# A four-layer graph network on one Trainium2 core: masks made early, mask bytes from the cast adjacency, keys centred in two operations, and three buffers or queues moved

## The chip, the core and the metric

The kernel runs on one core of one Trainium2 chip. The engines are TensorE (PE in the profile; its weight loads have a row of their own, PEld), VectorE (DVE), ScalarE (ACT), GpSimd (POOL) and SyncE (SP), which issues DMAs. DMAs are issued by SP, ACT and POOL, each in the order of its own queue. The metric is the device time of one execution in microseconds (us), lower is better. "L538" is line 538 of the kernel before.

## What is computed

Input are x (4096 nodes, 256 features) and adj (4096 x 4096, zeros and ones, about 0.8% ones). Four layers follow each other, each with a residual and a layernorm:

```python
x = layernorm(x + gat(x, W, b, a, adj))          # layer 0
x = layernorm(x + (diag(adj) + adj) @ (x @ w) + bias)   # layer 1
x = layernorm(x + two_steps(x, adj, W1, W2, W3, U1, U2)) # layer 2
x = layernorm(x + relu([x, mean_of_neighbours(x)] @ W + b)) # layer 3

# layer 0: 8 heads of 32 columns
logits[i, j, h] = leaky_relu(parent[i, h] + child[j, h], 0.2)
logits = where(adj[i, j] != 0, logits, 0)        # not minus infinity
out[i, h] = sum_j softmax_j(logits)[i, j, h] * feats[j, h]

# layer 2, twice: Xf = R @ Xf ; Xa = top_p_attention(Xa) @ Xa
# logits = (Xa W1' W2') (Xa W3')' ; keep the most probable 0.9 of each row
# Z += Xf @ U1[n].T + Xa @ U2[n].T
```

## The kernel before, in words

Nodes are handled in 32 blocks of 128 rows (NB). A scheduler of the framework puts the instructions of the Python program on each engine's queue, in an order of its own outside the parts marked as scheduled by hand; buffers of a pool are reused in rotation (`bufs`), and an instruction waits until the buffer it writes is free.

**Layer 0, sums0 (L404).** First the node features: for each pair of blocks (L443 to L483), x is loaded (SP, tile "x", three buffers), transposed by PE (L451), copied by ACT (L453), and multiplied with w0 (L457), whose logit columns DVE makes from the weights (L431, L432). `row_logits` stores one row of logits per head to memory (lpd).

Then the adjacency pass (L518 to L553): for each pair of blocks b, eight chunks g of four column blocks. Each chunk is loaded by SP into one of two "a" slots (L526), cast to the matmul's type by DVE (`ar`, L528, two buffers), turned to mask bytes by ACT (`nb`, L531, two instructions), which POOL stores to memory (`nad`, L532), and used by 32 matmuls of PE (L538). `factored` (L499 to L515) splits the weighted features of a block into three bf16 parts: DVE and ACT take turns (L503 to L513, tiles `vf` and `gb`, two buffers each), and ACT issues two stores per block (`gmd`, L515). The scheduler places these 32 blocks within 72 to 230 us. At the end of a pair, DVE combines the sums (`zt`, L547 to L552) and ACT stores them (`zd`, L553).

The mask of a chunk of attention (`mask`, L256 to L270) is: compare a row of logits with four column logits (DVE L261 for g of 2, 5, 7; otherwise ACT L267, a Sign), then one bitwise operation of DVE with the bytes (L263 or L269). `chunk0`, called near the end of the pass (L540), makes the mask of chunk 0 of head 0 ahead; it borrows both "a" slots, and its result is `gt0`, with the features in `gm0`.

**choose0 (L356)** branches on a value in memory (L358); all engines take part. Then the **attention loop** (L287 to L340): two halves of four heads; within a half, four tiles of 1024 rows (it); within it, four heads (hh); within a head, eight chunks g of 32 matmuls each (L320). At a tile's start SP loads bytes (`na`, L291) and, for it = 0, features (`gm`, L293) in the order of g. DVE reduces and normalises (L326 to L337). Layernorms that are due (`later`) are done one per head: DVE takes moments (L85, L86), POOL does the rest (L88, L89, L96), in tiles of two buffers (moments, L77).

**Layer 1 (L754)** multiplies by the adjacency, block by block (L787 to L799), with a layernorm on each (L798, tiles in the pool "l1w"; here DVE does L96 and POOL L88, L89). **Layer 2 (L802)** begins with `weights(0)` (L1519 to L1524: POOL issues loads of wt and affine) and `keys(0, X)`. `keys` (L877) transposes X (PE L901, ACT copies L902 to tile "e"), projects it (L906), and takes the moments of the keys: 32 matmuls (L923), DVE L924, PE L928, DVE L929 (`mom`). Then it centres them: for each of four parts of 1024 columns, DVE subtracts the mean in place (L935), ACT rounds to the matmul's type (L936, upper half of kT), and DVE takes the remainder (L937, lower half). PE's logits for the first rows (L979) read kT. `project` (L1445 to L1481) makes projections of two blocks; block 16 is projected before the centring, blocks 18 on in a loop (L1587). The main part of layer 2 (L1623 on) is scheduled by hand. Step 1 repeats keys. Layer 3 follows (L1845).

Of the kernel before, what the change touches and what calls it, by code (L numbers as in the profile page):

```python
# [9 lines left out]
F32 = mybir.dt.float32  # L10
I32 = mybir.dt.int32
F32R = mybir.dt.float32r
BF16 = mybir.dt.bfloat16
FP8 = mybir.dt.float8e4
# [9 lines left out]
P = 128  # L24
# [31 lines left out]
class Net:  # L56
# [19 lines left out]

    def moments(self, pool, src):  # L77

        nc = self.nc
        n = src.shape[1]  # L80
        stats = pool.tile([P, n, nc.vector.BN_STATS_DIM], F32, name="ln_stats")
        mv = pool.tile([P, n, nc.vector.BN_AGGR_DIM], F32, name="ln_mv")
        rstd = pool.tile([P, n], F32, name="ln_rstd")
        for q in range(n):
            nc.vector.bn_stats(stats[:, q, :], src[:, q, :])  # L85
            nc.vector.bn_aggr(mv[:, q, :], stats[:, q, :])  # L86
        var = pool.tile([P, n], F32, name="ln_var")
        nc.gpsimd.tensor_scalar_add(var, mv[:, :, 1], EPS)  # L88
        nc.gpsimd.tensor_tensor(rstd, var, self.power.to_broadcast([P, n]), ALU.pow)  # L89
        return mv, rstd  # L90

    def layernorm(self, pool, dst, src, engine=None):

        mv, rstd = self.moments(pool, src)
        for q in range(src.shape[1]):
            (engine or self.nc.vector).tensor_scalar(dst[:, q, :], src[:, q, :], mv[:, q, 0:1], rstd[:, q:q + 1],  # L96
                                                     op0=ALU.subtract, op1=ALU.mult)
# [117 lines left out]
    def layer0(self):  # L215
# [7 lines left out]
        with ExitStack() as ctx:  # L223
# [14 lines left out]
            first = pool.tile([P, IT], F32, name="lpb0")  # L238
            gt0 = pool.tile([P, 4, IT], FP8, name="gt0")
            gm0 = pool.tile([P, 4, 6 * C1], BF16, name="gm0")  # L240

# [5 lines left out]

            def chunk0(work):

                nc.sync.dma_start(gm0, gmd[0, :, 0:4, 0])  # L250
                na0, sg0 = (work.tile([P, 2, 4, P], F32, name="a", bufs=2).rearrange("p q k i -> p (q k i)").bitcast(U8)
                            .rearrange("p (k i) -> p k i", k=4) for _ in range(2))
                nc.sync.dma_start(na0, nad[0, :, 0:4, :])
                mask(gt0, sg0.bitcast(FP8), na0, first, 0, 0)

# [15 lines left out]

            self.sums0(both, nlc, fac, lpd, nad, zd, gmd, lambda: row_logits(first, 0, 0), chunk0)
            self.choose0(fac, zd, gmd, gm0)
# [13 lines left out]
            for half in range(2):  # L287
                for it in range(N // IT):
                    i0 = it * Q
                    for g in range(NB // K):  # L290
                        nc.sync.dma_start(na[:, g * K:(g + 1) * K], nad[it, :, g * K:(g + 1) * K, :])  # L291
                        if it == 0 and (half or g):
                            nc.sync.dma_start(gm[:, g * K:(g + 1) * K, 0], gmd[half, :, g * K:(g + 1) * K, 0])  # L293
# [8 lines left out]
                    for hh in range(H // 2):  # L302
# [5 lines left out]
                        for g in range(NB // K):  # L308

                            head0 = half == 0 and hh == 0 and g == 0  # L310
                            gt = gt0
                            if not head0 or it:
                                gt = work.tile([P, K, IT], FP8, name="gt", bufs=4)
                                sg = work.tile([P, K, IT], FP8, name="sg", bufs=3)
                                mask(gt, sg, na[:, g * K:(g + 1) * K, :], lpb, g, h)
                            for k in range(K):
                                jc = g * K + k
                                for q in range(Q):

                                    nc.tensor.matmul(acc[:, q, :6 * C1], gt[:, k, q * P:(q + 1) * P],  # L320
                                                     gm0[:, k, :] if head0 else gm[:, jc, hh, :],
                                                     start=(jc == 0 and q % 2 == 0),
# [15 lines left out]
                        for xs in later[:per_head]:  # L338
                            self.layernorm(work, xs, xs, nc.gpsimd)
                        del later[:per_head]  # L340
# [62 lines left out]

    def sums0(self, both, nlc, fac, lpd, nad, zd, gmd, then, chunk0):  # L404

# [5 lines left out]
        with ExitStack() as ctx:  # L411
# [31 lines left out]
            for b in range(0, NB, 2):  # L443
                two = slice(b, b + 2)
                x = work.tile([P, 2, D], F32, name="x", bufs=3)
                nc.sync.dma_start(x, xr[:, two, :])
                px = ps.tile([P, 512], F32, name="ps_x", bufs=2)
# [51 lines left out]
            def factored(b):  # L499
# [14 lines left out]
                for half in range(2):  # L514
                    nc.scalar.dma_start(gmd[half, :, b], gb[:, half * H // 2:(half + 1) * H // 2].rearrange("p h s c -> p h (s c)"))  # L515

            G = 4
            for b in range(0, NB, 2):  # L518
# [4 lines left out]
                for g in range(NB // G):  # L523
                    a = work.tile([P, 2, G, P], F32, name="a", bufs=2)
                    for q in range(2):
# [4 lines left out]
                    for q in range(2):  # L530
                        nc.scalar.mul(nb[:, :, q, :], a[:, q], float(FIFTH))  # L531
                    nc.gpsimd.dma_start(nad[it, :, g * G:(g + 1) * G, i:i + 2 * P], nb.rearrange("p g q i -> p g (q i)"))  # L532
                    for q in range(2):
                        for k in range(G):
                            jc = g * G + k
                            for s in range(2):
                                for t in range(2):
                                    nc.tensor.matmul(pz[q][:, t, :W], ar[:, q, k, :], src[:, jc, t, s],  # L538
                                                     start=(jc == 0 and s == 0), stop=(jc == NB - 1 and s == 1))
                if b == NB - 4:  # L540
                    chunk0(work)
                for q in range(2):
# [9 lines left out]
                    nc.vector.tensor_add(zt[:, 0], zt[:, 0], zt[:, 1])  # L552
                    nc.scalar.dma_start(zd[b + q], zt[:, 0])  # L553

# [199 lines left out]
    def layer1(self):  # L754
        nc, tc, NB, D, X = self.nc, self.tc, self.NB, self.D, self.X
        with self.ctx1 as ctx:
# [25 lines left out]
            for b in range(NB):  # L782
# [14 lines left out]
                nc.vector.tensor_add(xb[:, 0], xb[:, 0], row)  # L797
                self.layernorm(work, xb, xb)  # L798
                nc.gpsimd.dma_start(self.xd[b, :, 0, :], xb[:, 0])  # L799


    def layer2(self):  # L802
# [3 lines left out]
        with ExitStack() as ctx:  # L806
# [70 lines left out]
            def keys(step, src):  # L877
# [17 lines left out]
                for g in range(NB // 4):  # L895
# [23 lines left out]
                    for t in range(2):  # L919
                        nc.sync.dma_start(qd[t * A:(t + 1) * A, :, cols], qp)  # L920
                pm = ps1.tile([P, 512], F32, name="ps_r")
                for b in range(NB):
# [7 lines left out]

                project(step, 16)
                for c in range(N // 1024):
                    cols = slice(c * 1024, (c + 1) * 1024)
                    kc = qs[:A, cols]
                    nc.vector.tensor_scalar(kc, kc, mom[:A, 2 * A:], None, op0=ALU.subtract)  # L935
                    nc.scalar.copy(kT[:A, cols], kc)  # L936
                    nc.vector.tensor_sub(kT[A:, cols], kc, kT[:A, cols].bitcast(F32))  # L937
                pc = psum.tile([P, 512], F32, name="ps_tp")
# [580 lines left out]
            def weights(step):  # L1519

                ut = (self.u1t, self.u2t)[step]
                for i in range(2):
                    nc.gpsimd.dma_start(wt[:, :, i], ut[1 - i].rearrange("(c p) m -> p c m", p=P))
                nc.gpsimd.dma_start(affine, row_broadcast((self.ln_b, self.ln_g)[step], D))  # L1524

# [38 lines left out]
            for step in range(2):  # L1564
# [14 lines left out]
                for b in range(0, NB, 2):  # L1579
# [3 lines left out]
                    if edge:  # L1583
                        v = result(edge)
                        if v is not None:
                            rs[0], edge = v, None
                    if b:  # L1587
                        project(step, (b + 16) % NB)
# [367 lines left out]
```

## Time and profile before

| what | us |
|---|---|
| median of three executions | 4033.21 (4031.47 to 4039.32) |
| the profiled execution itself | 4036.06 |
| its span on the core | 4034.4 |
| PE busy | 3912.9 (97%) |
| DVE busy | 2994.1 (74%) |
| ACT busy | 2757.1 (68%) |
| POOL busy | 1088.5 (27%) |
| node features | 0 to 62 |
| adjacency pass | 72 to 600 |
| attention | 603 to 1327 |
| layer 1 | 1327 to 1625 |
| layers 2 and 3 | 1625 to 4034 |

The page sums busy time per engine over the span. The table of waits sums PE's idle time by the instruction that ended it. The timeline lists instructions in order of their start; the last bracket gives the idle time of the engine just before, and what released it. A row with "x32" joins 32 instructions in a row. The letter q after an engine (SPq) means its queue, where DMAs are issued. The granted clock of PE is 0.987 of full speed over the span.

### The profile page before, as it was taken

How to read it: one execution, taken by the hardware profiler on the slowest of the kernel's cores; microseconds unless marked ns; L12 is line 12 of the kernel's file. 1: busy time of each engine (PE TensorE's matmuls, PEld its weight loads, DVE VectorE, ACT ScalarE, POOL GpSimd, SP SyncE). 2: the span in 40 equal slices, each digit the busy share in tenths (PEclk: the TensorE clock that was granted, in tenths of full speed). 3: DMA queues.
4: the chain of work that ended last, by engine and by line, in shares of the span. 5: the costliest groups of instructions: out<-in, count | busy, mean ns of one | idle time of the engine just before them, and what ended most of it. 6: DMA issues, size and time to landing. Idle time of an engine off the chain costs nothing. (4 is left out here: it accounts for less than half of the span.)

```text
span 4034.4 us, 68767 instructions
## 1 busy us (share of the span) xinstructions
PE 3912.9 (97%) x25081; PEld 3383.5 (84%) x25081; DVE 2994.1 (74%) x6643; ACT 2757.1 (68%) x5127; POOL 1088.5 (27%) x1333
## 2 busy tenths in 40 slices
PE   8999999999999999899999999989999999999899
PEld 7899999999999788578888888865888888888687
DVE  7642328999999444567878788737899999999364
ACT  5543339999999322468888888825988888888132
POOL 0111110111333122301111111114555555555211
PEclk9999999999999999999999999999999999999999
DMA  4665547334222597432333232453333333335541
GB/s 136 224 214 175 178 147 228 93 101 131 69 76 64 192 369 311 131 115 95 98 97 101 95 104 92 146 190 100 103 116 103 106 119 99 107 120 188 185 152 47
DMA packets 320570, 556.42 MB, mean 138 GB/s; under 512 B 71558, under 2 KB 146198, under 8 KB 316118
## 3 DMA queue, kind: packets, MB, share of 16 engines
q1 hardware_dynamic: 239920, 395.13, 30.2%
q0 software_dynamic: 28336, 86.42, 6.5%
q10 hardware_dynamic: 51958, 70.29, 5.1%
q8 instruction: 203, 3.33, 0.3%
q14 instruction: 153, 1.25, 0.1%
HBM read 385.78 MB, written 165.94 MB: 137 GB/s over the span
## 5 line engine op out<-in xcount | busy, mean ns | idle before, releaser
L1345 PE MATMUL ps_a<-X,aT 128*128 128x256 f32 x4096 | 973.4, 380 | 1.3 <-ACT h L1486 1.1
L1345 PEld LDWEIGHTS ps_a<-X,aT 128*128 128x128 f32 x4096 | 776.5, 190 | 128.2 <-issue 3.5
L320 PE MATMUL acc<-gm,gt 128*128 128x198 bf16 x8192 | 706.2, 249 | 22.0 <-DMA gm<-gmd 6.8
L320 PEld LDWEIGHTS <-gt 128*128 128x128 fp8e4 x8192 | 702.8, 98 | 25.4 <-issue 9.8
L267 ACT ACTIVATE sg<-lpb,nlc 128x1024 fp8e4<-128x1024 f32 x636 | 667.2, 1135 | 61.5 <-DVE gt L269 39.8
L180 PE MATMUL ps_r<-XD,adj_piece 128*128 128x512 f32 x1888 | 528.4, 414 | 0.3 <-DMA adj_piece<-adjs 0.3
L538 PE MATMUL pz<-src,ar 128*128 128x264 f32 x4096 | 510.2, 287 | 15.2 <-DVE ar L528 12.7
L538 PEld LDWEIGHTS pz<-src,ar 128*128 128x128 f32 x4096 | 507.1, 190 | 18.1 <-DVE ar L528 11.6
L1072 ACT ACTIVATE ja<-e,nc 128x2048 uint8<-128x2048 f32 x240 | 480.9, 2004 | 2.0
L1338 ACT COPY aT<-ps_tp 128x512 f32<-128x512 f32 x512 | 296.4, 579 | 222.5 <-PE ps_tp L1336 220.5
L180 PEld LDWEIGHTS ps_r<-XD,adj_piece 128*128 128x128 f32 x1888 | 332.9, 189 | 69.3 <-issue 12.9
L531 ACT ACTIVATE nb<-a 128x512 uint8<-128x512 f32 x256 | 156.4, 630 | 287.7 <-DMA a<-in_adjt_dram 274.7
L1137 DVE MAX8 cand<-v 128x8 f32<-128x256 f32 x1024 | 347.3, 412 | 4.4
L1187 DVE SCALAR_TENSOR_TENSOR e<-e,edge 128x512 f32<-128x512 f32 x512 | 347.3, 750 | 2.2
L1336 PE MATMUL ps_tp<-ident,e 128*128 128x128 f32 x2048 | 307.9, 273 | 0.0
L1133 DVE SCALAR_TENSOR_TENSOR v<-e,hi 128x2048 f32<-128x2048 f32 x128 | 300.7, 2350 | 2.4
L1336 PEld LDWEIGHTS ps_tp<-ident,e 128*128 128x128 f32 x2048 | 257.1, 142 | 51.4 <-issue 0.7
L261 DVE TENSOR_SCALAR sg<-lpb,nlc 128x1024 fp8e4<-128x1024 f32 x384 | 285.4, 779 | 5.9 <-DVEq L358 3.9
L979 PE MATMUL ps_logit<-kT,q 128*128 128x512 f32 x1024 | 276.8, 412 | 12.4 <-DVE kT L937 8.0
L981 ACT ACTIVATE e<-ps_logit 128x1024 f32<-128x1024 f32 x256 | 260.2, 1027 | 30.3 <-PE ps_logit L979 30.3
L528 DVE CAST ar<-a 128x1024 fp32r<-128x1024 f32 x128 | 88.6, 693 | 231.0 <-PE pz L538 229.9
L790 PE MATMUL ps_adj<-XD,adj_piece 128*128 128x512 f32 x1024 | 244.9, 399 | 0.0
(397 smaller groups left out, 5543.7 us busy)
## 6 DMA issues: line engine op xcount, KB each, us to landing
adj_piece<-adjs SPq DMA_DIRECT2D x552, 256.0 KB, 2.7
a<-in_adjt_dram SPq DMA_DIRECT2D x256, 256.0 KB, 3.0
adjs<-adj_piece SPq DMA_DIRECT2D x96, 512.0 KB, 4.8
na<-nad SPq DMA_DIRECT2D x64, 512.0 KB, 3.7
nad<-nb POOLq DMA_DIRECT2D x128, 128.0 KB, 3.3
lpb<-lpd POOLq DMA_DIRECT2D x32, 512.0 KB, 4.1
na<-nad ACTq DMA_DIRECT2D x16, 1024.0 KB, 6.9
gmd<-gb ACTq DMA_DIRECT2D x64, 198.0 KB, 3.3
```

The source lines that it names most:

```text
L180: nc.tensor.matmul(ps, a[:, k, :], rhs(jc).rearrange("p s d -> p (s d)"), start=(jc == 0), stop=(jc == self.NB - 1))
L261: nc.vector.tensor_scalar(sg[:, k, :], lpb, nlc[:, 4 * g + k, h:h + 1], 2.0 ** -5, op0=ALU.is_ge, op1=ALU.mult, saturate=False)
L267: nc.scalar.activation(sg[:, k, :], lpb, AF.Sign, scale=-1.0, bias=nlc[:, 4 * g + k, h:h + 1], saturate=False)
L320: nc.tensor.matmul(acc[:, q, :6 * C1], gt[:, k, q * P:(q + 1) * P], gm0[:, k, :] if head0 else gm[:, jc, hh, :], start=(jc == 0 and q % 2 ...
L538: nc.tensor.matmul(pz[q][:, t, :W], ar[:, q, k, :], src[:, jc, t, s], start=(jc == 0 and s == 0), stop=(jc == NB - 1 and s == 1))
L1072: nc.scalar.activation(ja, e[:, s * HALF:(s + 1) * HALF], f, bias=nc1, accum_out=fs[:, i + s:i + s + 1])
L1133: nc.vector.scalar_tensor_tensor(v, ec, hi, ec, op0=ALU.is_lt, op1=ALU.mult, accum_out=sb[:, s:s + 1])
L1137: nc.vector.max(cand[:, 8 * j:8 * j + 8], v[:, k * 256:(k + 1) * 256])
L1187: nc.vector.scalar_tensor_tensor(ec, ec, edge[:, j:j + 1], ec, op0=ALU.is_ge, op1=ALU.mult)
L1336: nc.tensor.transpose(pt[:, k * P:(k + 1) * P], e[:, jc * P:(jc + 1) * P], self.ident)
L1338: nc.scalar.copy(aT, pt)
L1345: nc.tensor.matmul(pa[:, :D], aT[:, k * P:(k + 1) * P], X[:, jc, :], start=(jc == 0), stop=(jc == NB - 1))
```

## The change

1. x is loaded into the "a" slots, four blocks to a tile by two DMAs; the tile "x" is gone. "a" still has two buffers.
2. nb is made from ar, the cast adjacency, and not from a.
3. POOL and not ACT issues the gmd stores of `factored`.
4. `early_mask` takes the place of `chunk0`: it makes the masks of chunks 0 and 1 of head 0 in four parts of two column blocks, at b = 20 to 26, by DVE alone, in the tiles "nf" and "v"; `gt0` and `gm0` hold eight column blocks and not four.
5. In the attention loop's first tile, SP loads chunks 2 to 7 first and then 0 and 1; chunks 0 and 1 of the first head use gt0 and gm0; `gm` of chunk 0 is loaded in both halves.
6. The layernorm tiles of `later` in the attention loop have six buffers.
7. The last two zd stores are issued by SP.
8. Layer 1's layernorm on each block takes its tiles from the pool "l1" (one buffer by default, two for these tiles).
9. In `keys`, ACT makes the upper half of kT by an Identity with the negated mean as its bias, straight from qs; DVE makes the lower half in one operation (subtract the mean, subtract the upper half). `project` of blocks 16 and 18 stands ahead of the moments.
10. `weights(0)` is issued by SP and not by POOL; `weights(1)` as before.

```diff
-    def moments(self, pool, src):
+    def moments(self, pool, src, bufs=2):
...
-        stats = pool.tile([P, n, nc.vector.BN_STATS_DIM], F32, name="ln_stats")
+        stats = pool.tile([P, n, nc.vector.BN_STATS_DIM], F32, name="ln_stats", bufs=bufs)
...
+            def early_mask(work, part):
+
+                if part == 0:
+                    nc.sync.dma_start(gm0, gmd[0, :, 0:8, 0])
+                two = slice(2 * part, 2 * part + 2)
+                na0, sg0 = (work.tile([P, 2, H, C1], F32, name=name).rearrange("p s h c -> p (s h c)")[:, :512]
+                            .bitcast(dt).rearrange("p (k i) -> p k i", k=2) for name, dt in (("nf", U8), ("v", FP8)))
+                nc.sync.dma_start(na0, nad[0, :, two, :])
+                for k in range(2):
+                    nc.vector.tensor_scalar(sg0[:, k, :], first, nlc[:, 2 * part + k, 0:1], 2.0 ** -5,
+                                            op0=ALU.is_ge, op1=ALU.mult, saturate=False)
+                bits = [t.rearrange("p k i -> p (k i)").bitcast(U32) for t in (gt0[:, two, :], sg0, na0)]
+                nc.vector.tensor_tensor(*bits, ALU.bitwise_and)
...
-                    for g in range(NB // K):
+                    begun = 2 if it == half == 0 else 0
+                    for g in [*range(begun, NB // K), *range(begun)]:
                         nc.sync.dma_start(na[:, g * K:(g + 1) * K], nad[it, :, g * K:(g + 1) * K, :])
-                        if it == 0 and (half or g):
+                        if it == 0:
                             nc.sync.dma_start(gm[:, g * K:(g + 1) * K, 0], gmd[half, :, g * K:(g + 1) * K, 0])
...
-                            head0 = half == 0 and hh == 0 and g == 0
-                            gt = gt0
-                            if not head0 or it:
+                            head0 = g < 2 and half == it == hh == 0
+                            if head0:
+                                gt = gt0[:, g * K:(g + 1) * K, :]
+                            else:
...
-                            self.layernorm(work, xs, xs, nc.gpsimd)
+                            self.layernorm(work, xs, xs, nc.gpsimd, bufs=6)
...
-                x = work.tile([P, 2, D], F32, name="x", bufs=3)
-                nc.sync.dma_start(x, xr[:, two, :])
+                if b % 4 == 0:
+                    x4 = work.tile([P, 2, 4, P], F32, name="a").rearrange("p q k i -> p (q k i)").rearrange(
+                        "p (b d) -> p b d", d=D)
+                    for q in range(0, 4, 2):
+                        nc.sync.dma_start(x4[:, q:q + 2], xr[:, b + q:b + q + 2, :])
+                x = x4[:, b % 4:b % 4 + 2]
...
-                    nc.scalar.dma_start(gmd[half, :, b], gb[:, half * H // 2:(half + 1) * H // 2].rearrange("p h s c -> p h (s c)"))
+                    nc.gpsimd.dma_start(gmd[half, :, b], gb[:, half * H // 2:(half + 1) * H // 2].rearrange("p h s c -> p h (s c)"))
...
-                        nc.scalar.mul(nb[:, :, q, :], a[:, q], float(FIFTH))
+                        nc.scalar.mul(nb[:, :, q, :], ar[:, q].bitcast(F32), float(FIFTH))
...
-                if b == NB - 4:
-                    chunk0(work)
+                if NB - 12 <= b < NB - 4:
+                    early_mask(work, (b - NB + 12) // 2)
...
-                    nc.scalar.dma_start(zd[b + q], zt[:, 0])
+                    (nc.sync if b == NB - 2 else nc.scalar).dma_start(zd[b + q], zt[:, 0])
...
-                self.layernorm(work, xb, xb)
+                self.layernorm(pool, xb, xb)
...
+                for b in (16, 18):
+                    project(step, b)
                 pm = ps1.tile([P, 512], F32, name="ps_r")
...
-                project(step, 16)
+                minus = kept[:A, 130:131]
+                nc.vector.tensor_scalar_mul(minus, mom[:A, 2 * A:], -1.0)
                 for c in range(N // 1024):
                     cols = slice(c * 1024, (c + 1) * 1024)
-                    kc = qs[:A, cols]
-                    nc.vector.tensor_scalar(kc, kc, mom[:A, 2 * A:], None, op0=ALU.subtract)
-                    nc.scalar.copy(kT[:A, cols], kc)
-                    nc.vector.tensor_sub(kT[A:, cols], kc, kT[:A, cols].bitcast(F32))
+                    nc.scalar.activation(kT[:A, cols], qs[:A, cols], AF.Identity, bias=minus)
+                    nc.vector.scalar_tensor_tensor(kT[A:, cols], qs[:A, cols], mom[:A, 2 * A:], kT[:A, cols].bitcast(F32),
+                                                   op0=ALU.subtract, op1=ALU.subtract)
...
-                ut = (self.u1t, self.u2t)[step]
+                ut, queue = ((self.u1t, nc.sync), (self.u2t, nc.gpsimd))[step]
                 for i in range(2):
-                    nc.gpsimd.dma_start(wt[:, :, i], ut[1 - i].rearrange("(c p) m -> p c m", p=P))
-                nc.gpsimd.dma_start(affine, row_broadcast((self.ln_b, self.ln_g)[step], D))
+                    queue.dma_start(wt[:, :, i], ut[1 - i].rearrange("(c p) m -> p c m", p=P))
+                queue.dma_start(affine, row_broadcast((self.ln_b, self.ln_g)[step], D))
...
-                    if b:
+                    if b > 2:
                         project(step, (b + 16) % NB)
```

More of the change, by code (lines that the diff above doesn't have):

```diff
@@ L75, in constants @@
         self.diagr = pool.tile([P, self.NB], F32R, name="diagr")
-    def moments(self, pool, src):
+    def moments(self, pool, src, bufs=2):
         nc = self.nc
         n = src.shape[1]
-        stats = pool.tile([P, n, nc.vector.BN_STATS_DIM], F32, name="ln_stats")
-        mv = pool.tile([P, n, nc.vector.BN_AGGR_DIM], F32, name="ln_mv")
-        rstd = pool.tile([P, n], F32, name="ln_rstd")
+        stats = pool.tile([P, n, nc.vector.BN_STATS_DIM], F32, name="ln_stats", bufs=bufs)
+        mv = pool.tile([P, n, nc.vector.BN_AGGR_DIM], F32, name="ln_mv", bufs=bufs)
+        rstd = pool.tile([P, n], F32, name="ln_rstd", bufs=bufs)
         for q in range(n):
@@ L86, in moments @@
             nc.vector.bn_aggr(mv[:, q, :], stats[:, q, :])
-        var = pool.tile([P, n], F32, name="ln_var")
+        var = pool.tile([P, n], F32, name="ln_var", bufs=bufs)
         nc.gpsimd.tensor_scalar_add(var, mv[:, :, 1], EPS)
@@ L90, in moments, with layernorm @@
         return mv, rstd
-    def layernorm(self, pool, dst, src, engine=None):
-        mv, rstd = self.moments(pool, src)
+    def layernorm(self, pool, dst, src, engine=None, bufs=2):
+        mv, rstd = self.moments(pool, src, bufs)
         for q in range(src.shape[1]):
@@ L238, in layer0 @@
             first = pool.tile([P, IT], F32, name="lpb0")
-            gt0 = pool.tile([P, 4, IT], FP8, name="gt0")
-            gm0 = pool.tile([P, 4, 6 * C1], BF16, name="gm0")
+            gt0 = pool.tile([P, 8, IT], FP8, name="gt0")
+            gm0 = pool.tile([P, 8, 6 * C1], BF16, name="gm0")
             nad = self.nad
@@ L246, in layer0 @@
             gmd = dram.tile([2, P, NB, H // 2, 6 * C1], BF16, name="gmd")
[L248 to L254, printed above, removed]
+            def early_mask(work, part):
[10 more added lines that the diff above has]
+                nc.vector.tensor_tensor(*bits, ALU.bitwise_and)
             def mask(gt, sg, na, lpb, g, h):
@@ L270, in mask @@
                                                    op0=ALU.logical_shift_right, op1=ALU.bitwise_and)
-            self.sums0(both, nlc, fac, lpd, nad, zd, gmd, lambda: row_logits(first, 0, 0), chunk0)
+            self.sums0(both, nlc, fac, lpd, nad, zd, gmd, lambda: row_logits(first, 0, 0), early_mask)
             self.choose0(fac, zd, gmd, gm0)
@@ L320, in layer0 @@
                                     nc.tensor.matmul(acc[:, q, :6 * C1], gt[:, k, q * P:(q + 1) * P],
-                                                     gm0[:, k, :] if head0 else gm[:, jc, hh, :],
+                                                     gm0[:, jc, :] if head0 else gm[:, jc, hh, :],
                                                      start=(jc == 0 and q % 2 == 0),
@@ L402, in factors0, with sums0 @@
         nc.scalar.dma_start(self.fits, fits)
-    def sums0(self, both, nlc, fac, lpd, nad, zd, gmd, then, chunk0):
+    def sums0(self, both, nlc, fac, lpd, nad, zd, gmd, then, early_mask):
         nc, tc, NB, D, N = self.nc, self.tc, self.NB, self.D, self.N
@@ L523, in sums0 @@
                 for g in range(NB // G):
-                    a = work.tile([P, 2, G, P], F32, name="a", bufs=2)
+                    a = work.tile([P, 2, G, P], F32, name="a")
                     for q in range(2):
```

## The prediction, made before the result was known

> **What bounds the kernel now.** I read the page's busy times first, then the table of what TensorE waited for, then busy time by stage, then the timeline at each wait.
>
> ```profile
> span 4034.4 us, 68767 instructions
> PE 3912.9 (97%) x25081; PEld 3383.5 (84%) x25081; DVE 2994.1 (74%) x6643; ACT 2757.1 (68%) x5127; POOL 1088.5 (27%) x1333
> ```
>
> TensorE (PE) is busy 97%, and the change leaves its instruction count alone. What can be won is PE's idle time, 4034.4 - 3912.9 = 121.5 us, plus matmuls that run slow after an idle. The waits (us in total, times, longest), those the change touches:
>
> ```profile
> PE pz L538 <- DVE ar L528: 12.7, 8, 3.1
> PE ps_logit L979 <- DVE kT L937: 8.0, 3, 3.8
> ...
> PE acc L320 <- DMA gm<-gmd: 6.8, 1, 6.8
> PE ps_nf L457 <- ACT xT L453: 6.6, 2, 6.1
> ...
> PE acc L320 <- ACTq L358: 6.0, 1, 6.0
> PE acc L320 <- DVE gt L263: 4.6, 3, 2.8
> PE acc L320 <- DVE gt L269: 4.5, 3, 2.1
> ...
> PE ps_tp L906 <- ACT e L902: 4.1, 1, 4.1
> ```
>
> 53 us in all; the rest (adj_piece loads, layer 1's start, the tail) the change doesn't touch. Busy time by stage, adjacency pass and then attention (window: its length, then busy time of PE, PEld, DVE, ACT, POOL):
>
> ```profile
> 85.00:610.00 525.00, 502.95 (x4041) 499.25 (x4039) 211.31 (x431) 208.44 (x343) 98.62 (x131) 0.99 0.58 191
> ...
> 625.00:1340.00 715.00, 700.20 (x8109) 695.82 (x8107) 683.63 (x891) 655.08 (x631) 166.77 (x143) 0.99 0.34 101
> ```
>
> In the first, DVE and ACT have room; in the second DVE is at 96%, so a wait on DVE reaches PE.
>
> **Slow matmuls after an idle.** [...] 32 matmuls of L320 take 2.90 us warm, but
>
> ```profile
> 564.36 1.88 PE L538 MATMUL pz<-src,ar 128*128 128x264 f32 x7 [3.05 <-DVE ar L528]
> ...
> 603.45 5.37 PE L320 MATMUL acc<-gm,gt 128*128 128x198 bf16 x32 [6.04 <-ACTq L358]
> 615.59 6.66 PE L320 MATMUL acc<-gm,gt 128*128 128x198 bf16 x58 [6.78 <-DMA gm<-gmd]
> ```
>
> 5.37 after 6.04 idle. Idles of 2.82 to 4.07 us cost 1.5 to 1.9 more afterwards (L320 at 1263: x32 in 4.55); one of 2.59 (169.01) cost nothing. So an idle cut below 2.6 us pays some 1.7 extra.
>
> **The change, part by part** (gain: value taken, and bounds).
>
> *Start: 2 (0 to 4).* ACT now issues four nb (L531) from 8.82 to 13.3, each behind an adjacency load, before the first xT copy (13.22), though ps_x was ready near 7. They go: with x in the "a" slots no adjacency tile is loaded early. But L457 also needs w0's logit columns, whose DVE chain (L431/L432) ends near 12.8: L457 can move from 13.84 to about 11.8. The two early ar casts (.69 each) go back into the loop, where DVE has room. The first adjacency loads wait for an x slot, free near 52 us by the transposes' times, 20 us before L538 starts.
>
> *Adjacency pass, 119 to 220: 6 (-8 to 11).* Ten waits of L538, 11.8 us. ACT's nb waits for the adjacency DMA (274.7 us of ACT idle on the page), with gb copies queued behind it in order; DVE's vf waits for gb, with the ar cast queued behind. Reading ar, nb waits for no DMA, and the a slot is freed by the DVE cast alone. In exchange ar (two buffers) waits for nb too, and POOL issues the 64 gmd stores as well as nad. POOL per chunk of 4.1 us (32 matmuls of .127, as x64 in 8.09 at 169 shows): nad .75, two gmd 1.5. It fits; nad can stand 1.5 behind gmd. The loop over gb is the tight one: casts and subtractions .63 + .85 + .63, nb 1.2, cast .6, issue .85, landing 3.5 (median there) = 8.3 us per two blocks, against 9.5 available (37 chunks for 32 blocks from 72 to 230). Slack 1.2. The early masks put 8 x .78 + 4 x .6 = 8.6 us of DVE there (one chunk's cast may be 3.4 late before PE notices: 4.1 less its own .69). Their five loads stand in SP's queue, each behind a store of POOL that lands some 5.6 us after its block's cast; an adjacency load behind them, wanted 8.2 (two chunks) after that cast, lands at 5.6 + 3.5 = 9.1, .9 late, inside the 3.4. Half the gain is kept.
>
> [...] Here nad's issue takes .75 beside DVE's casts and lands after 3.3, gmd from ACT after 3.3: no such delay for the one per chunk. That is why I stay near the low price.
>
> *Mask of chunk 0: 4.5 (3 to 4.6).* It took both "a" slots at 554, so the load for the last blocks was issued only at 559.85: 3.05 idle, 1.5 cold. Neither slot is taken now. One mask (four L267 of 1.1 on ACT, L269 1.22) leaves this place; what replaces it is counted above.
>
> *First chunks of attention: 5 (2 to 8).* The branch wait stays (DVE ends at 599.34, 3.9 to branch); the last two zd stores go from ACT's queue to SP's, .35 each ahead of a branch that DVE sets: nothing. Chunk 0 runs 603.45 to 608.8; then PE waited for gm of chunk 1 until 615.59, and chunk 7 ended at 636.45. Now chunk 1 is ready and runs to 611.7. Chunk 2 needs na and gm, now first in SP's queue: .7 MB instead of 1.2 MB, at 341 GB/s of a saturated DMA 1.5 us earlier, 614. Idle 2.3, warm; 6 x 2.9 = 17.4 gives 631.4, against 636.45.
>
> *Layernorm buffers: 8 (4 to 10.8).* With two buffers DVE's L86 waits for POOL's L96:
>
> ```profile
> 1072.84 0.18 DVE L86 BATCH_NORM_AGGREGATE ln_mv<-ln_stats 128x2 f32<-128x6 f32 x1 [1.03 <-POOL X L96]
> ...
> 1076.39 0.25 DVE L86 BATCH_NORM_AGGREGATE ln_mv<-ln_stats 128x2 f32<-128x6 f32 x2 [2.33 <-POOL X L96]
> ...
> 1082.77 1.59 PE L320 MATMUL acc<-gm,gt 128*128 128x198 bf16 x10 [2.06 <-DVE gt L269]
> ```
>
> 3.4 us of DVE in each of three places, and PE loses 2.2, 3.7 and 3.2, with rounding 9.2, plus 1.65 cold. Six buffers take the wait away. DVE per head is 21.4 to 22.4 against PE's 21.9, so part may return; I keep 8 of 10.8.
>
> *Seam of layers 1 and 2: 5.5 (4 to 6).*
>
> ```profile
> 1629.93 1.93 ACT L902 COPY e<-ps_logit 128x1024 f32<-128x1024 f32 x2 [19.79 <-DVE X L96]
> ```
>
> This copy waited for the last layernorm because its tile overlaps the layernorm's; and that was late since POOL issued wt loads (.73 and .77, from 1627.02) between its steps. Both go: the copy waits for L901, done near 1626.0, and L906 starts near 1627.2, not 1631.00: 3.8, plus 1.8 cold (x4 in 3.78, not 1.97). wt is issued by SP after L96 (about 1627.5) and is first used near 1643; adj_piece loads behind it were issued at 1629.85. Hidden; without that cover, 1.5.
>
> *Keys: 5 (3 to 6.5) in step 0, 3 (1 to 5) in step 1.*
>
> ```profile
> 1667.85 3.07 DVE L935 TENSOR_SCALAR e<-e,v 64x1024 f32<-64x1024 f32 x3
> 1670.95 4.57 DVE L937 TENSOR_TENSOR kT<-e,kT 64x1024 fp32r<-64x1024 f32 x3
> 1672.22 3.35 PE L979 MATMUL ps_logit<-kT,q 128*128 128x512 f32 x7 [3.76 <-DVE kT L937]
> ```
>
> Three subtractions stood before the first L937. Now after L929: a sign change .2, ACT's Identity with bias about 1.1, DVE's one operation about 1.28. [...] L267, of that form, shows 1.135. For DVE, L1187 (512: .75) and L1133 (2048: 2.35) give 1.28 at 1024. With L929 and L940, kT is ready 3.2 us after L928. In step 0 PE has 2.9 us of work to put there (L1547 of the projections moved ahead, seven matmuls, L939 and L942; their copies on ACT and DVE move with them, into time in which both wait for the moments): idle .4 instead of 3.76 + .46 + .31 + .52, and 1.9 cold gone; I take 5 of 6.5. In step 1 only L939/L942 (.75) stand there: idle 2.2 instead of 4.2, below the 2.6 at which the clock held: 2 + 1.9, taken as 3.
>
> **Sum.** 2 + 6 + 4.5 + 5 + 8 + 5.5 + 5 + 3 = 39. The profiled execution took 4036.06 us (4034.4 of span and 1.7 around it), 2.85 over the median of the runs, 4033.21. 4036.06 - 39 = 3997.1; less 2.85: 3994.
>
> **Rivals.**
> *Absorbed.* For: DVE is at 96% in attention, DMA is saturated after 603, and in-order queues let a stall reappear one instruction on. Start 0, pass 0, mask 4.5, chunks 3, layernorms 4, seam 5.5, keys 3 + 1 (still cold in step 1) = 21: 4012. Against: each wait has its releaser on record and it goes.
> *All of it.* Every term at its better end: 4 + 11 + 4.6 + 8 + 10.8 + 6 + 6.5 + 5 = 56: 3977.
> *POOL's queue decides (slower).* Two gmd issues stand between nad stores, in order, and each block's gb is freed by their landing. If [...] landing lengthens by d, each two blocks lose d - 1.2, 16 times over. The other parts give 33, so it is level at d = 3.3 and slower by .2% from d = 3.8. At d = 4.2, 48 lost: 4048. Against: nad's .75 and 3.3 above.
>
> **Numbers.** Likeliest .62 (own range 3982 to 4006), absorbed .24, all .05, POOL .06, and .03 in which POOL's loss just cancels the rest. A measurement of this kernel tells about .2% (8 us) from no change: faster .91, same .03, slower .06. The range, 3977 to 4018, leaves out POOL's cases and the edges.
>
> **What would show it.** Right: L531 without DMA waits and no ten waits of L538 before 230; none at 564; L86 without waits for POOL; L320's chunk 2 near 614; L906 by 1628 less what was gained; L979 after under 1 us in step 0 and under 2.6 in step 1. Wrong: gmd landing over 5 us from POOL, L521 waits (gb) above 1.5; new DVE waits in attention; L979 still cold.

## The result and the profile after

| what | before | after |
|---|---|---|
| median (of four executions each), us | 4035.32 | 4007.32 |
| lowest to highest | 4031.47 to 4039.32 | 4002.08 to 4011.93 |
| the profiled execution | 4036.06 | 4011.93 |
| its span | 4034.4 | 4010.2 |

The ratio is 0.9932, 95% interval 0.9916 to 0.9947: 28 us faster, where 39 were forecast (3994 on the scale of the first three runs; 4007 lies in the range, and just outside the 3982 to 4006 of the likeliest case). The profiled execution of the changed kernel is the slowest of its four, so the traces show a difference of only 24.2 us of span. Lines of the changed kernel are up to 14 higher: L538 is now L550, L528 L540, L509 to L513 are L521 to L525, L320 is L328, L937 L950 and L979 L993.

The page of the changed kernel, busy time:

```profile
span 4010.2 us, 68765 instructions
PE 3906.8 (97%) x25081; PEld 3377.3 (84%) x25081; DVE 2990.2 (75%) x6647; ACT 2742.6 (68%) x5119; POOL 1136.7 (28%) x1394
```

PE's idle time is 4010.2 - 3906.8 = 103.4 us, 18.1 less than before. What PE waited for (us in total, times, longest):

```profile
PE pz L550 <- DVE ar L540: 18.6, 10, 3.7
...
PE acc L328 <- DVEq L366: 5.6, 1, 5.6
PE acc L328 <- DMA gm<-gmd: 5.4, 1, 5.4
...
PE ps_nf L469 <- issue: 3.7, 1, 3.7
...
PE acc L328 <- DVE gt L275: 3.0, 2, 1.7
```

The waits for masks fell from 9.1 to 3.0, those for kT and for the copy at the head of layer 2 (8.0 and 4.1) are gone from the head of the list. But the first line grew: the waits for the cast adjacency, 12.7 before, are 18.6, although the mask of chunk 0, 3.05 of them, is gone. The time between landmarks that both traces have (start of the first instruction of a line) tells where the 24 us come from:

| stretch, before / after | before | after | gain | forecast |
|---|---|---|---|---|
| start to L457 / L469 | 13.84 | 11.56 | 2.3 | 2 |
| features, to L538 / L550 | 58.58 | 60.36 | -1.8 | 0 |
| adjacency pass, to L320 / L328 | 531.03 | 539.32 | -8.3 | 10.5 |
| attention, to L746 / L758 | 724.06 | 712.98 | 11.1 | 13 |
| layer 1, to L901 / L913 | 297.48 | 300.66 | -3.2 | 0 |
| layer 2 step 0, to its last L1345 / L1359 wait | 996.35 | 983.37 | 13.0 | 10.5 |
| step 1, to L1540 / L1554 of the tail | 1137.09 | 1130.13 | 7.0 | 3 |
| the rest | 275.97 | 271.82 | 4.1 | 0 |

Outside the adjacency pass every stretch lies within 4.1 us of its forecast. The pass should have gained 10.5 (6 and 4.5) and lost 8.3. PE in that pass, in the changed kernel's timeline:

```profile
123.11 9.63 PE L550 MATMUL pz<-src,ar 128*128 128x264 f32 x64 [2.63 <-DVE ar L540]
132.90 4.17 PE L550 MATMUL pz<-src,ar 128*128 128x264 f32 x32 [0.17 <-DVE ar L540]
140.37 21.39 PE L550 MATMUL pz<-src,ar 128*128 128x264 f32 x160 [3.30 <-DVE ar L540]
162.93 8.11 PE L550 MATMUL pz<-src,ar 128*128 128x264 f32 x64 [1.17 <-DVE ar L540]
172.53 4.19 PE L550 MATMUL pz<-src,ar 128*128 128x264 f32 x32 [1.49 <-DVE ar L540]
180.38 25.62 PE L550 MATMUL pz<-src,ar 128*128 128x264 f32 x192 [3.65 <-DVE ar L540]
...
233.01 372.65 PE L550 MATMUL pz<-src,ar 128*128 128x264 f32 x3040 [0.43 <-DVE deg L561]
```

From 233 on nothing waits: the 3.05 of the mask of chunk 0 are gone as forecast. From 100 to 233 there are twelve waits, 20.2 us, where the kernel before had 11.8; after the one of 2.63 the next 64 matmuls take 9.63 instead of 8.10. The trace has the granted clock at half for 3.41 us four times in this part, once in the kernel before; by estimate (three more stretches, half of each) that is some 5 us more. Who waits ahead of them is read from ACT's waits in this part (72 to 230 us before, 72 to 235 after), first before, then after:

```profile
ACT nb L531 <- DMA a<-in_adjt_dram: 44.9, 30, 4.1
ACT gb L509 <- DMA gmd<-gb: 8.6, 11, 1.7
```

```profile
ACT gb L521 <- DMA gmd<-gb: 39.1, 17, 4.3
ACT gb L523 <- DVE vf L522: 14.7, 21, 1.3
ACT nb L543 <- DVE ar L540: 11.4, 14, 1.8
```

The wait for the adjacency DMA is gone, as forecast. In its place ACT waits for gmd: the store that frees a gb buffer.

### The profile page after: what moved, and what is told of

It is laid out like the page before. It is cut to its first block, busy times and chain, and to the rows that moved or that the text cites. A ratio compares the mean times of both kernels' runs of the same rounds, so it can differ in the third digit from the quotient of the medians.

```text
span 4010.2 us, 68765 instructions
## 1 busy us (share of the span) xinstructions
PE 3906.8 (97%) x25081; PEld 3377.3 (84%) x25081; DVE 2990.2 (75%) x6647; ACT 2742.6 (68%) x5119; POOL 1136.7 (28%) x1394
## 5 line engine op out<-in xcount | busy, mean ns | idle before, releaser
L1359 PE MATMUL ps_a<-X,aT 128*128 128x256 f32 x4096 | 970.4, 379 | 1.3 <-ACT h L1500 1.1
L1359 PEld LDWEIGHTS ps_a<-X,aT 128*128 128x128 f32 x4096 | 774.1, 190 | 127.2 <-issue 3.3
L328 PE MATMUL acc<-gm,gt 128*128 128x198 bf16 x8192 | 702.5, 248 | 14.2 <-DVEq L366 5.6
L328 PEld LDWEIGHTS <-gt 128*128 128x128 fp8e4 x8192 | 700.4, 97 | 16.2 <-issue 11.3
L550 PE MATMUL pz<-src,ar 128*128 128x264 f32 x4096 | 513.5, 288 | 20.6 <-DVE ar L540 18.6
L550 PEld LDWEIGHTS pz<-src,ar 128*128 128x128 f32 x4096 | 510.3, 191 | 23.7 <-DVE ar L540 21.3
L543 ACT ACTIVATE nb<-ar 128x512 uint8<-128x512 f32 x256 | 147.5, 623 | 268.4 <-DVE ar L540 265.2
L993 PE MATMUL ps_logit<-kT,q 128*128 128x512 f32 x1024 | 274.1, 409 | 4.0 <-ACT e L995 1.7
L540 DVE CAST ar<-a 128x1024 fp32r<-128x1024 f32 x128 | 88.9, 695 | 248.1 <-PE pz L550 242.4
```

The lines of the kernel that those rows point to most:

```text
L1359: nc.tensor.matmul(pa[:, :D], aT[:, k * P:(k + 1) * P], X[:, jc, :], start=(jc == 0), stop=(jc == NB - 1))
```

## The experiments

Theory A: gmd on POOL's queue lands too late; ACT's gb cast waits for the buffer, DVE's vf for that cast, and the cast of the adjacency stands behind vf on DVE. Theory B: the same loop, but it is the new order of ACT's and DVE's instructions and not the queue. Theory C: the early masks on DVE, or ar's buffers. Ratios are to the kernel before, with 95% intervals; the changed kernel's own is 0.9932. With intervals of this width two ratios are told apart from some 9 us on; where two runs differ by less, the argument rests on their traces. The scheduler orders the instructions anew in each kernel, so an edit can also move instructions that it doesn't name.

**gmd issued by ACT again.**

```diff
-                    nc.gpsimd.dma_start(gmd[half, :, b], ...
+                    nc.scalar.dma_start(gmd[half, :, b], ...
```

> The changed kernel, with the gmd stores issued by ACT again. In the changed kernel ACT's first gb cast (L521) waits 39 us for gmd landings between 72 and 235 us, against 9 before the change, and TensorE's waits for the cast adjacency in the pass sum to 20 us against 12. Theory A (POOL's queue: the store lands 0.6 us later and stands in order with nad): with ACT issuing, the waits of L521 fall to about 10 us, TensorE's waits in the pass to 8 or less, and the time to about 3995 us (8 to 14 below the changed kernel). Theory B (two gb buffers are too few for the new order of casts, whoever issues): waits of L521 stay above 25 us and the time stays within 4 us of the changed kernel, 4007.

4001.24 us, ratio 0.9913 (0.9896 to 0.9929). ACT's waits for gmd fell from 39.1 to 16.8, PE's for the cast (and its neighbours on DVE) from 20.1 to 10.6. The pass takes 525.9 us, against 539.3 in the changed kernel, though the times alone (7.7 us by the ratios) don't tell the two apart. By the traces the queue is a part of it, and not all: the waits stay above what A expected.

**Three gb buffers.**

```diff
-                gb = work.tile([P, H, 3, 2 * C1], BF16, name="gb")
+                gb = work.tile([P, H, 3, 2 * C1], BF16, name="gb", bufs=3)
```

(with xT and one small tile of factors0 in vf's buffers, for room)

> The changed kernel with three gb buffers in place of two; the tile xT takes the buffers of vf for room. Theories A and B: a third buffer gives each landing about 4 us more, waits of L521 fall under 5 us, and TensorE loses less than 6 us in the pass in place of 20 and of some 5 of slow matmuls after long waits: 3988 to 3993 us. Theory C (the early masks on DVE or the ar buffers, which now wait for ACT too, are what holds the cast up): waits of TensorE in the pass stay above 14 us and the time above 4001.

3988.66 us, ratio 0.9871 (0.9855 to 0.9887), as A and B expected; PE's waits in the pass are 10.8, more than expected. C is out as the main cause: the early masks and ar's two buffers are still there.

**nb from a again, gmd on POOL.**

```diff
-                        nc.scalar.mul(nb[:, :, q, :], ar[:, q].bitcast(F32), float(FIFTH))
+                        nc.scalar.mul(nb[:, :, q, :], a[:, q], float(FIFTH))
```

> The changed kernel with the mask bytes made from the loaded adjacency again and not from the cast one. As the prediction had it (nb from ar takes ACT off the adjacency DMA): ACT's waits for that DMA come back, 40 us and more, on top of those for gmd, and the time is 4 to 10 us above the changed kernel, 4011 to 4017. Theory A or B alone (the landing of gmd is what ends last in the loop): nb's source does not matter, within 3 us of 4007.

4007.52 us, ratio 0.992 (0.9903 to 0.9937): no difference from the changed kernel that the time can tell (the pass takes 538.6 us, against 539.3). The waits only changed names, ACT's in 72 to 235 us:

```profile
ACT nb L543 <- DMA a<-in_adjt_dram: 33.5, 23, 3.3
ACT gb L523 <- DVE vf L522: 15.3, 24, 1.3
ACT gb L521 <- DMA gmd<-gb: 7.7, 12, 1.4
```

So in the changed kernel making nb from ar, for which the forecast gave 6 us, brings nothing that the time or the trace shows. That doesn't say that it is worth nothing, as the last experiment but one shows.

**Both cures: gmd on ACT and three gb buffers.**

> The changed kernel with both: gmd issued by ACT and three gb buffers. If the landing of gmd is the whole of the loss, either cure removes it and both together give no more than the better one, within 4 us: 3986 to 3993 us. If the two act on different waits (POOL's order holds up nad, the buffers hold up gb), both together are 5 us or more below each.

3977.98 us, ratio 0.9851 (0.9834 to 0.9867), 10.7 below the better of the two (8 by the ratios; the four executions of the one all lie below those of the other): "either cure removes it" fell. PE's and ACT's waits:

```profile
PE pz L552 <- DVE ar L542: 1.6, 1, 1.6
PE pz L552 <- DVE big L390: 0.4, 1, 0.4
```

```profile
ACT gb L523 <- DMA gmd<-gb: 0.9, 2, 0.5
```

The pass is now all but free of waits. From L552's start to the start of attention it takes 505.6 us, against 539.3 in the changed kernel and 531.0 before.

**Two layernorm buffers in attention.**

```diff
-                            self.layernorm(work, xs, xs, nc.gpsimd, bufs=6)
+                            self.layernorm(work, xs, xs, nc.gpsimd)
```

> The changed kernel with two buffers again for the layernorm tiles in attention. As predicted (DVE's wait for POOL reaches TensorE): the waits of DVE L86 for POOL come back, 3.4 us in three places, TensorE waits 8 to 10 us for masks between 1060 and 1270 in place of 3.0, and the time is 6 to 10 us above the changed kernel, 4013 to 4017. Rival (attention is bound by DVE's work, the wait was hidden in it): within 2 us of 4007.

4016.19 us, ratio 0.9952 (0.9936 to 0.9968), some 8 us slower than the changed kernel; the intervals overlap, the attention stage is 6.6 us longer in the trace. DVE waits 10.1 us for POOL again, in six places; PE's waits for masks are back:

```profile
PE acc L328 <- DVE gt L269: 5.8, 3, 2.8
PE acc L328 <- DVE gt L275: 2.9, 3, 2.1
```

8.7 in place of 3.0, plus slow matmuls after the two of 2.8 (32 in 4.55 us, where 32 at 1080.99 take 2.91). DVE's 96% didn't swallow it: the forecast 8 fits, the rival "hidden in DVE's work" falls.

**Keys in three operations.**

```diff
-                    nc.scalar.activation(kT[:A, cols], qs[:A, cols], AF.Identity, bias=minus)
-                    nc.vector.scalar_tensor_tensor(kT[A:, cols], ...
+                    kc = qs[:A, cols]
+                    nc.vector.tensor_scalar(kc, kc, mom[:A, 2 * A:], None, op0=ALU.subtract)
+                    nc.scalar.copy(kT[:A, cols], kc)
+                    nc.vector.tensor_sub(kT[A:, cols], kc, kT[:A, cols].bitcast(F32))
```

> The changed kernel with the keys centred in three operations again (the two projections stay ahead of the moments). As predicted: L993's first matmuls wait about 1 to 2 us in step 0 (fillers hide 2.9) and 3.5 in step 1, where a slow clock follows; the time is 4 to 8 us above the changed kernel. Rival (the projections moved ahead did it all): step 0 unchanged, only step 1 loses, 2 to 4 us above.

4014.40 us, ratio 0.9947 (0.993 to 0.9963), about 6 slower (the intervals overlap; its seven executions spread from 4008.63 to 4027.39). Step 0 waits 1.79 and 1.04, with 8 matmuls in 3.78 in place of 2.51; step 1 waits 2.81, with 12 in 5.49 in place of 4.80. Both steps lose, as predicted; the projections moved ahead did not do it alone. In the profiled execution, at 4023.35 the second slowest of the seven, more is lost than the waits: in step 0 four groups of sixteen matmuls of L965, between 1664.88 and 1685.80, take 3.78 each (those of L966, the same line in the changed kernel, 2.05), with no wait among them, and step 0 takes 18.3 us longer than in the changed kernel.

**The seam of layers 1 and 2 undone.**

```diff
-                self.layernorm(pool, xb, xb)
+                self.layernorm(work, xb, xb)
...
-                ut, queue = ((self.u1t, nc.sync), (self.u2t, nc.gpsimd))[step]
+                ut, queue = ((self.u1t, nc.gpsimd), (self.u2t, nc.gpsimd))[step]
```

> The changed kernel with layer 1's layernorm tiles in the old pool and the first weights of layer 2 loaded by POOL again. As predicted: the copy at the head of layer 2 waits for the last layernorm again, TensorE 4.1 us, with 1.8 of slow matmuls after it: 5 to 6 us above the changed kernel, 4012 to 4013. Rival (a wait of TensorE for key work comes in any case a little later): under 3 us.

4013.28 us, ratio 0.9939 (0.9921 to 0.9958). The interval is too wide to tell 3 from 6, or from nothing. The trace shows L918 waiting 2.93 in place of 0.27, and its first four matmuls in 2.88 in place of 1.98: 3.6 us. The slow rate lasts into the next matmuls (eight of L913 in 1.87 in place of 1.04), and the stretch of layer 2's step 0 is 5.2 us longer, near the 5.6 between before and after.

**The first head's z on SP's queue.**

```diff
-                        nc.gpsimd.dma_start(z, zd[i0:i0 + Q, :, h]...
+                        (nc.sync if h + it == 0 else nc.gpsimd).dma_start(z, zd[i0:i0 + Q, :, h]...
```

> The changed kernel with the first head's z load (1024 pieces of 132 bytes) issued by SP and not by POOL at the start of attention. In the changed kernel the features of chunk 2 land 11.5 us after their issue, as those of chunk 1 did before the change though more bytes stood ahead of them then. Theory D (small pieces of other queues share the DMA engines with gm, so the place in SP's queue matters little): z comes later, gm of chunk 2 lands 1 to 3 us earlier, and the time falls by 1 to 3 us. Theory E (bytes in flight set it): z's 132 KB of 3.9 MB matter nothing, gm within 0.5 us of 11.5.

4006.64 us, ratio 0.9929 (0.9911 to 0.9947): nothing that the time can tell. In the trace chunk 2 starts 10.1 us after chunk 0 in place of 13.0, and attention takes 709.1 in place of 713.0. PE waits 3.03 for the features of chunk 2 in place of 5.44, as D expects; but with z on POOL's queue two other runs show 9.8 (three gb buffers) and 10.4 (nb from a) between the two chunks, so D is not shown, and the 4 us of one trace are not shown in the time.

**32 bytes.** In both runs with three buffers the pass's matmuls ran faster where nothing waits, 1657 or 1658 in 200 us against 1635. I took the operands' places for the cause.

```diff
-                lpT = work.tile([H, 2 * P], F32, name="lpT", bufs=1)
+                lpT = work.tile([H, 2 * P + 8], F32, name="lpT", bufs=1)[:, :2 * P]
```

> The changed kernel with one small tile made 32 bytes longer, so that v, vf, gb, ar and nb lie 32 bytes further on; no instruction and no order changes. In the two runs with three gb buffers the 4096 matmuls of the adjacency pass took 120.7 ns each where nothing waits (1657 in 300 to 500 us), in all others 122.3 (1635); there src and ar start at 0 and 32 modulo 64 bytes, in the others at equal remainders. Theory F (where the two operands lie sets it): 1657 matmuls in that window and 6 to 7 us off the pass and the time. Rival (the rate comes from something else in those two kernels): 1635, time as the changed kernel.

4007.86 us, ratio 0.9917 (0.9901 to 0.9934), 1641 matmuls in that window: theory F, which expected 1657, isn't borne out, all the less as the run after next has tiles of the same sizes as the run with both cures and shows 1646. What sets the 1.4% stays open; by estimate (4096 matmuls, 1.6 ns each) it is worth about 7 us of the 29 by which both cures beat the changed kernel.

**Both cures and z on SP.**

> Both cures of the pass (gmd issued by ACT, three gb buffers) and the first head's z loads issued by SP. If z's effect (3.8 us between the start of attention and that of layer 1 in the profile of the run with z alone) is real and adds: 3974 us against 3978 for the two cures alone, and gm of chunk 2 waits under 3 us. Rival: z only moves a wait, 3977 to 3981.

3976.44 us, ratio 0.9848 (0.9831 to 0.9864): not to be told from both cures alone; chunk 2 waits 2.78. It has the lowest median measured here.

**Both cures, nb from a.**

> Both cures of the pass, but with the mask bytes made from the loaded adjacency and not from the cast one. With two gb buffers the source made no difference (4007.5 us). Theory G (it does once gmd no longer ends last): ACT waits for the adjacency DMA again, TensorE over 5 us in the pass, the time 5 to 12 us above the two cures, 3983 to 3990. Rival (the source never mattered): 3976 to 3981.

3997.84 us, ratio 0.9899 (0.9883 to 0.9916): 20 us slower than with nb from ar. ACT waits for the adjacency again, and PE for the casts behind:

```profile
ACT nb L545 <- DMA a<-in_adjt_dram: 42.9, 30, 4.2
```

```profile
PE pz L552 <- DVE ar L542: 12.2, 11, 2.0
PE pz L552 <- DVE deg L563: 4.1, 4, 2.5
```

The same edit that did nothing in the changed kernel is worth 20 us here; some 3 of them are the slower rate of the matmuls (1646 against 1657). G holds, and more strongly than expected.

**Only gmd on POOL, in the kernel before.**

```diff
-                    nc.scalar.dma_start(gmd[half, :, b], ...
+                    nc.gpsimd.dma_start(gmd[half, :, b], ...
```

> The kernel before, with the gmd stores issued by POOL: this one part of the change alone. Theory A (POOL's queue is what costs): TensorE's waits in the pass rise from 12 to 18 us or more and the time by 6 to 12 us, ratio 1.0015 to 1.003. Theory B (the new order of casts costs, not the queue): ratio within 0.001 of 1.

4042.93 us, ratio 1.0013 (1.0006 to 1.002), about 5 us slower, a little less than A expected and more than B, and PE's waits rise as A expects:

```profile
PE pz L538 <- DVE ar L528: 18.0, 12, 3.2
PE pz L538 <- DVE deg L549: 2.3, 1, 2.3
```

But ACT's waits (72 to 235 us) are not those of theory A:

```profile
ACT gb L511 <- DVE vf L510: 20.7, 29, 1.4
ACT gb L509 <- DMA gmd<-gb: 9.1, 14, 1.7
```

Its wait for gmd is 9.1, as before the edit (8.6); what grew is its wait for DVE. So this edit costs by itself, but not by the path that A names. Nor is this the old order: the first cast of the next block stands ahead of the last cast of this one at 5 of the 31 places where two blocks meet, in the kernel before at 19. Queue and order are not separated by this run. With ACT issuing, the changed kernel still waited 16.8 for gmd against 8.6 before, so the queue isn't all of it.

## Why the prediction came out as it did

*The number: in the range, and partly by luck.* The pass missed its forecast by 18.8 us, in the trace. Alone, that would have left 20 of the 39, about 4013: still in the range, but the number of the case "absorbed" and not of the likeliest. Step 1 and the tail gained 8.1 more than forecast, for no reason that the forecast had, and made up for part of it.

*Start: right in place, lost again.* L469 starts at 11.56, 2.3 earlier (2 forecast); the features up to the pass then take 1.8 longer. I don't know why.

*Adjacency pass: the step that failed.* "The loop over gb is the tight one ... 8.3 us per two blocks, against 9.5 available. Slack 1.2." The loop was the right one and its length wrong. Means over the 32 blocks of the changed kernel's trace: from the start of a block's first cast (L521) to the end of its last (L525) it is 4.5 us, where the forecast's casts, subtraction and nb sum to 3.9; from there until both stores have landed it is 5.3, where issue and landing were taken at .85 + 3.5. Together 9.75 per two blocks, so there was no slack. L521 starts every 5.2 us (70.0 to 230.0) and waits for gmd at 17 blocks, up to 4.3: the sign "L521 waits (gb) above 1.5". One place in the timeline:

```profile
121.08 0.63 ACT L521 CAST gb<-vf 128x528 bf16<-128x528 f32 x1 [4.26 <-DMA gmd<-gb]
121.61 0.63 ACT L525 CAST gb<-vf 128x528 bf16<-128x528 f32 x1
...
122.37 0.68 DVE L540 CAST ar<-a 128x1024 fp32r<-128x1024 f32 x1
...
122.53 1.17 POOL L527 DMA_DIRECT2D gmd<-gb  x2 [5.19 <-ACT gb L525]
...
127.40 0.63 ACT L521 CAST gb<-vf 128x528 bf16<-128x528 f32 x1 [2.64 <-DMA gmd<-gb]
```

Here ACT's first cast of the next block (L521, at 121.08) stands ahead of the last cast of this one (L525, at 121.61), and waits for the store of the block before. So that store's landing holds up L525, hence this block's own store, hence the next landing: from L525 over the issue (122.53, two of .54 and more, behind nad) to the landing that frees L521 at 127.40 it is 5.8 us. This order lengthens the loop where it stands, but the change did not bring it: it stands at 9 of the 31 places where two blocks meet, with 10.3 of the 39.1 us of waits; before at 19, and in the kernel with both cures, where ACT waits .9 for gmd, at 21. The landing was off by less than it seems: 3.9 us from POOL, taken at 3.5. The 3.3 of the kernel before are the median of the 8 landings, of 64, that its trace has; issued by POOL in the kernel before they took 3.4, by ACT in the changed kernel 3.5 (medians, 72 to 235 us).

The runs show that a third buffer and ACT's queue together take the waits away. They don't show every link between: the kernel before took a block each 5.4 us, no faster, with PE waiting 11.8 in place of 20.2. The forecast's slower rival named this loop and this path ("each block's gb is freed by their landing"), but with the same slack of 1.2, which wasn't there. The term measured -13 (-8.3, less the 4.5 of the mask and .5 at the branch), below the bound of -8 that I gave.

POOL's issue of a gmd store takes .54, counted at .75, and ACT's in the kernel before .34 (medians). The rival of POOL's queue needed landings longer by 3.3 to be level; they were .6 longer by the medians of 3.9 and 3.3 (the latter of 8 landings). What sets those .6, no run separates.

*Mask of chunk 0: right.* No wait between 233 and 605.

*First chunks of attention: forecast 5, about 1.*

```profile
611.24 7.53 PE L328 MATMUL acc<-gm,gt 128*128 128x198 bf16 x64 [5.58 <-DVEq L366]
...
624.21 5.98 PE L328 MATMUL acc<-gm,gt 128*128 128x198 bf16 x42 [5.44 <-DMA gm<-gmd]
```

Chunk 1 is ready, as said. But chunk 2's features land 13.0 us after chunk 0's start, not 10.5: "in SP's queue .7 MB instead of 1.2 MB, 1.5 us earlier" failed. gm took 11.5 us from its issue, as before the change (11.3), with less ahead of it. So the bytes ahead in its own queue alone did not set it; what else did is not shown. And after 5.44 idle the clock is lost again: half for 6.83 us from 622.1 on.

*Layernorm buffers: right*, 8 forecast; the attention stage gained 11.1, some 1.2 of it from the first chunks, and undoing it alone cost 8 (6.6 in the trace).

*Seam: right*, 5.5 forecast. From L901 to the end of the first four matmuls of L906 it was 9.8, now 4.2 (5.6).

```profile
1626.02 1.93 ACT L914 COPY e<-ps_logit 128x1024 f32<-128x1024 f32 x2 [15.99 <-PE ps_logit L913]
1627.09 1.98 PE L918 MATMUL ps_tp<-e,wkq 128*128 128x512 f32 x4 [0.27 <-ACT e L914]
1627.35 0.90 SPq L1537 DMA_DIRECT2D wt<-in_u1t_dram  x2
```

*Keys: right in step 0; in step 1 the wait went, and the slow clock stayed.* Step 0: no wait for kT is left, where .4 was forecast. Step 1: I counted .75 of work ahead of L993; the built order also puts 16 matmuls of L966 there, and nothing waits for kT:

```profile
2716.73 4.26 ACT L949 ACTIVATE kT<-e,v 64x1024 fp32r<-64x1024 f32 x4 [3.72 <-DVE v L946]
2717.44 3.44 PE L966 MATMUL ps_tp<-v,e 64*128 64x128 f32 x16 [0.32 <-DVE v L957]
2717.91 4.87 DVE L950 SCALAR_TENSOR_TENSOR kT<-e,v,kT 64x1024 fp32r<-64x1024 f32 x4 [0.53 <-ACT kT L949]
2720.80 4.80 PE L993 MATMUL ps_logit<-kT,q 128*128 128x512 f32 x12
```

But L993 is still slow, a sign named for being wrong: its first twelve take 4.80 (5.23 before), the sixteen of L966 3.44 (2.05 before). The clock is at half for 6.83 us from 2717.8 on, as long as before. From the end of the moments to the sixteenth matmul of the logits it was 13.8 us and is 11.8: 2.0 gained, where 2 + 1.9 was taken as 3.

*The clock: 2.6 us is not the limit.* The forecast let a wait below 2.6 us keep the clock. The trace before already has one of 1.87 (at 119.38) with half clock after it, the trace after one of 2.22 (at 221.96). The last section sets the clock beside PE's idle time.

*What no step forecast.* Layer 1, in which only the layernorm's tiles were moved, took 3.2 longer in this trace: the same waits for XD cost 4.00 and 3.15 in place of 3.20 and 3.73, one of 1.19 is new, and eight matmuls of L781 take 3.78 in place of 2.98 at the half clock. Its 300.7 us are no more than spread: it takes 300.5 in the run with only gmd on POOL, whose layer 1 is that of the kernel before (297.5). Step 1 gained 5 beyond the keys, and the rest 4. Of step 1's, 3.4 fall ahead of its keys: from the last L1345 wait to the last L1345 of step 0 it is 86.3 us, 89.7 before, with 3.4 us at half clock in place of 10.2. In four other traces with the changed kernel's instructions there (nb from a, two layernorm buffers, z on SP, 32 bytes) this piece takes 86.6 to 90.8, so the gain is within the spread. The rest takes 272.6 in the run with only gmd on POOL, where it is as in the kernel before, against 276.0 there: of this gain too at most a part is the change's.

## What to carry to other kernels

When a buffer is freed by a store, add up its whole loop: from the first write to the last, and from there until every store has landed; measure both, and see in which order each engine's queue holds the instructions. Here 8.3 us per two blocks were counted, 9.75 measured. A wait taken away on one engine is worth what the next wait in the same loop leaves of it: nb from ar gave nothing with two gb buffers and 20 us with three and gmd on ACT. So undo each part of a change by itself, and again after the next bound has been lifted, and look whether the edit has reordered anything else.

## What the runs showed of the hardware that was not expected

In the traces of the kernels before and after, the times at which the granted clock of TensorE changed lie multiples of 3.41 us apart, and it was at half for 3.41 or 6.83 us at a time (the last time, at the end of the trace, aside). From 72 to 597 us, the adjacency pass for the most part, these two traces have 19 stretches of 3.41 us between such times that are at full clock and in which PE idled 0.7 us or more. After the 5 with 2.04 to 3.00 us of idle time the clock was at half in the next stretch; after the 12 with 0.72 to 1.82 it was not; after the 2 with 1.87, once. A wait of 2.22 us that lay within one stretch was followed by half clock, one of 2.59 that two stretches shared was not. First the changed kernel (wait from 219.73 to 221.96), then the kernel before (166.42 to 169.01); the numbers are busy times of PE, PEld, DVE, ACT and POOL, the clock, and the DMAs' share and GB/s:

```profile
219.30:222.70 3.40, 1.18 (x10) 0.96 (x9) 3.16 (x6) 2.67 (x6) 2.08 (x3) 1.00 0.20 57
222.70:226.10 3.40, 3.40 (x18) 3.40 (x17) 1.82 (x5) 0.92 (x2) 1.82 (x3) 0.50 0.94 292
...
164.90:168.30 3.40, 1.52 (x13) 1.31 (x11) 2.33 (x5) 2.83 (x5) 0.75 (x1) 1.00 0.18 48
168.30:171.70 3.40, 2.69 (x22) 2.69 (x23) 3.16 (x8) 1.16 (x3) 0.75 (x1) 1.00 0.81 247
```

These counts are of this part alone: in step 1 of the changed kernel the clock fell at 2717.8 after a stretch in which PE was busy 2.39 of 3.40 us, with narrow matmuls (64 to 129 columns); and in the run with keys in three operations the matmuls stayed slow from 1664.88 to 1685.80 with no wait of PE in between.

The pass's matmuls (128x264, fp32r), at full clock and with no wait, took 122.3 ns each in the kernels before and after (1635 in 200 us), 120.7 with three gb buffers (1657), 121.5 with three and nb from a (1646) and 121.9 with tiles shifted by 32 bytes (1641), for the same PE instructions. The cause is open. A DMA of 198 KB in pieces of 396 bytes took 11.3 and 11.5 us from issue to use while queue q0, that of POOL's issues, took 33.5% and 34.2% of the DMA engines' time (603 to 618 us before, 611 to 626 after), in the one case behind 1.0 MB in its own queue, in the other behind 0.5 MB.
